# A three-pass graph kernel on one core: producers two blocks or groups ahead, node sums a block behind, sigmoid in place, and gather buffers that divide the number of groups

## The chip, the cores and the metric

The kernel runs on one core of a Trainium2 chip. The metric is the device time of one execution in microseconds (us); the median of 14 executions of the kernel before is 36074.31 us, the lowest 36034.74 and the highest 36114.28. Engines are named as in the profile: PE is TensorE (matmul), PEld its weight loads, DVE VectorE, ACT ScalarE, POOL GpSimd, SP SyncE.

## The reference, cut to what matters

Two layers of a graph network over 30,000 nodes with 128 features and 960,000 edges, which are sorted by destination. Everything is float32.

```python
def _rel_graph_conv(h, basis, coeff, bias, src, dst, etype, norm):   # R = 32 types, B = 8 bases
    W = jnp.einsum('rb,bdf->rdf', coeff, basis)
    Hr = jnp.einsum('nd,rdf->nrf', h, W)
    msg = Hr[src, etype] * norm
    return jax.ops.segment_sum(msg, dst, num_segments=N) + bias

h = relu(layernorm(x))
h1 = relu(_rel_graph_conv(h, basis1, coeff1, bias1, ...))
x = x + _rel_graph_conv(h1, basis2, coeff2, bias2, ...)

h = relu(layernorm(x))
for t in range(4):                       # 4 edge types
    k, q, v = h @ Wk[t] + bk[t], h @ Wq[t] + bq[t], h @ Wv[t] + bv[t]
    eta = jax.nn.sigmoid(k[dst] + q[src])
    msg = jnp.where((edge_type == t)[:, None], eta * v[src], 0.0)
    outs.append(segment_sum(msg, dst) + h @ Ws[t] + b[t])
x = x + mean(outs)
```

## The kernel before

The edges are walked three times: once for each of the two relational convolutions (passes c1 and c2, `rel_body`) and once for the gated layer (`gate_body`). Between c1 and c2 a short stage makes the node features of the second convolution, and between c2 and the gate another makes two tables: `ktab` with a key per node and type, and `qvtab` with query and value per node and type. Passes c1, c2 and the gate take nearly the whole span.

**Tiles, groups, blocks, stages.** A tile is 128 edges. `G` = 3 tiles are a group, whose destinations lie in one window of `W` = 32 nodes. `S` = 5 groups are a block, `SB` = 5 blocks a stage, `NQ` = 4 stages one iteration of the loop (`tc.For_i`): `NS` = 20 blocks, `NG` = 100 groups, 300 tiles. `NI` = 25 iterations make a pass. The body of an iteration is unrolled, and each engine keeps the order in which the code is written (`manual_schedule`), so a line that stands later in the text stands later in its engine's queue.

**Between the engines** there are only data dependencies and buffers: a tile name with `bufs=n` has n buffers that are used in turn, and whoever writes a buffer waits until all readers of its last content are done. The loop is the staggered kind: at each `stage_boundary()` (every fifth block) an engine may go on into the next stage only when all engines have passed `leave_stage()` of the stage that it is in, which stands at that stage's third block. An engine can so run at most 15 groups ahead across such a boundary, and across the end of an iteration.

**A group of the relational pass** (loop from L369). GpSimd gathers the rows of the three tiles' source nodes into `hg` (12 buffers), an indirect DMA of 128 rows each (helper, L107). VectorE makes for each tile a scatter matrix `sb` (L394, 9 buffers): one of 32 window columns per edge, times the edge's eight basis coefficients. TensorE multiplies `hg` with `sb` and adds the three tiles up in `pa` (L400, 3 buffers in PSUM). ScalarE copies `pa` into the block's `ab` (L404).

**Once per block**, written between the groups of that block:
- `types(s)` (L337): SP loads the edge types, 256 KB, into `er`.
- `onehot(s)`: VectorE compares them into `oh` (L344), TensorE multiplies by the coefficient table into `pc` (L347, one buffer).
- `coefficients(s)` (L356): VectorE multiplies `pc` with the edge weights into `ce`, which `sb` reads.
- `bases_out(s)` (L364): TensorE takes the block's `ab` through the eight bases into `po` (two buffers).
- `add_windows(po, base, s)` (L323): VectorE adds the five windows of `po` to the node sums `agg`, which stay in SBUF; the start columns come from registers that `bases` loads once per stage.

Before the change a block s has `types(s + 1)` at its start; `bases_out(s - 1)` after its second group; `add_windows` of block s - 1, `onehot(s + 1)` after its third; `coefficients(s + 1)` after its fourth.

**A group of the gate.** SP loads the keys of the group's window (`kw`, L437) and once per block the codes of the edges (`kb`, L429, 960 KB), which VectorE turns into one-hots in place (L441) along with `sel` (L446). `keys(n)`: TensorE picks each edge's key into `pk` (L453, 3 buffers in PSUM). GpSimd gathers query and value together into `qv` (9 buffers). VectorE adds the query to `pk` (L493), ScalarE takes the sigmoid into `eta` (L495, two buffers in PSUM), and `sums(n)` multiplies by the value into `msg` (L461) and adds to the block's `po` on TensorE (L463). At group n the text has, in order: the gathers of n, `keys(n + 1)`, the add and the sigmoid of n, `sums(n - 1)`; then, at the block's second group, `add_windows` of the block before, and at its third `onehot(s + 1)`.

Of the kernel before, what the change touches and what calls it, by code (L numbers as in the profile page):

```python
# [18 lines left out]
P = 128  # L19
# [44 lines left out]
def kernel(  # L64
# [210 lines left out]
    def sorted_path():  # L275
        with ExitStack() as all_:
# [48 lines left out]
            def rel_body(table, bas, cof):  # L325
                def body(i, io, pool, ps, iw, ic):
                    stage = {}
                    er, oh, pc, ce, ab, po, base = {}, {}, {}, {}, {}, {}, {}

                    def loads(k):  # L330
                        stage[k] = [stage_tile(io, "idx", src, I32, i, k),
                                    stage_tile(io, "relc", reld, F32, i, k),
                                    stage_tile(io, "nrm", norm, F32, i, k, 4 * TQ - S * G)]

                    def types(s):
                        er[s] = pool.tile([P, TQ, TP], I32, name="er")
                        nc.sync.dma_start(  # L337
                            er[s].rearrange("p c e -> p (c e)"),
                            bass.AP(tensor=et32_row.tensor, offset=(i * NG + s * S) * GE,
                                    ap=[[TQ * TP, 4], [0, R], [1, TQ * TP]]))  # L340

                    def onehot(s):
                        oh[s] = pool.tile([P, TQ, TP], F32, name="oh")
                        nc.vector.tensor_scalar(oh[s], er[s], icol4, None, op0=ALU.is_equal)  # L344
                        pc[s] = ps.tile([TP, TQ, 4, B], F32, name="pc", bufs=1)
                        for c in range(TQ):
                            nc.tensor.matmul(pc[s][:, c].rearrange("p q b -> p (q b)"),  # L347
                                             lhsT=oh[s][:, c, :],
                                             rhs=cof.rearrange("p q b -> p (q b)"),
                                             start=True, stop=True)  # L350

                    def coefficients(s):
                        ce[s] = pool.tile([TP, 4, TQ, B], F32, name="ce")
                        t0 = s % SB * S * G
                        nrm = stage[s // SB][2][:, t0:t0 + 4 * TQ]
                        nc.vector.tensor_mul(  # L356
                            ce[s], pc[s].rearrange("p c q b -> p q c b"),
                            nrm.rearrange("p (q c) -> p q c", q=4).unsqueeze(3).to_broadcast(
                                [TP, 4, TQ, B]))

                    def bases_out(s):
                        po[s] = ps.tile([P, S, W], F32, name="po")
                        for b in range(B):
                            nc.tensor.matmul(po[s].rearrange("p s w -> p (s w)"),  # L364
                                             lhsT=bas[:, b, :],
                                             rhs=ab[s][:, b].rearrange("p s w -> p (s w)"),
                                             start=(b == 0), stop=(b == B - 1))

                    loads(0)  # L369
                    types(0)  # L370
                    onehot(0)
                    coefficients(0)
                    for s in range(NS):
                        k = s // SB
                        if s % SB == 0:
                            if s:
                                tc.stage_boundary()
                            if k + 1 < NQ:
                                loads(k + 1)
                        if s % SB == 2:  # L380
                            leave_stage()
                        idx, relc, _ = stage[k]
                        if s + 1 < NS:
                            types(s + 1)
                        ab[s] = pool.tile([P, B, S, W], F32, name="ab")
                        for g in range(S):
                            t0 = (s % SB * S + g) * G
                            hg = pool.tile([TP, G, D], F32, name="hg", bufs=12)
                            for j in range(G):
                                gather(hg[:, j, :], table, idx[:, t0 + j:t0 + j + 1])  # L390
                            pa = ps.tile([P, B, W], F32, name="pa", bufs=3)
                            for j in range(G):
                                sb = pool.tile([TP, B, W], F32, name="sb", bufs=9)
                                nc.vector.scalar_tensor_tensor(  # L394
                                    sb, iw[:TP].unsqueeze(1).to_broadcast([TP, B, W]),
                                    relc[:, t0 + j:t0 + j + 1],
                                    ce[s].rearrange("p q c b -> p (q c) b")[
                                        :, g * G + j, :].unsqueeze(2).to_broadcast([TP, B, W]),
                                    op0=ALU.is_equal, op1=ALU.mult)
                                nc.tensor.matmul(pa.rearrange("p b w -> p (b w)"),  # L400
                                                 lhsT=hg[:, j, :],
                                                 rhs=sb.rearrange("p b w -> p (b w)"),
                                                 start=(j == 0), stop=(j == G - 1))
                            nc.scalar.copy(ab[s][:, :, g, :], pa)  # L404
                            if g == 1 and s:
                                bases_out(s - 1)
                            if g == 2 and s:
                                add_windows(po[s - 1], base[(s - 1) // SB], s - 1)
                            if g == 2 and s % SB == 0:
                                base[k] = bases(i, k, DVE)  # L410
                            if g == 2 and s + 1 < NS:
                                onehot(s + 1)
                            if g == 3 and s + 1 < NS:
                                coefficients(s + 1)
                    bases_out(NS - 1)
                    add_windows(po[NS - 1], base[NQ - 1], NS - 1)
                return body

            def gate_body(i, io, pool, ps, iw, ic):
                stage = {}  # L420
                kb, kw, sel, pk, qv, eta, po, base, kbase = {}, {}, {}, {}, {}, {}, {}, {}, {}

                def loads(k):
                    stage[k] = [stage_tile(io, *a, i, k) for a in (
# [14 lines left out]
                def onehot(s):  # L439
                    flat = kb[s].rearrange("p g e -> p (g e)")  # L440
                    nc.vector.tensor_tensor(flat, flat, ic.to_broadcast([P, S * G * TP]),  # L441
                                            ALU.is_equal)
                    sel[s] = pool.tile([TP, S * G, W], F32, name="sel")
                    t0 = s % SB * S * G
                    relc = stage[s // SB][1][:, t0:t0 + S * G]
                    nc.vector.tensor_tensor(  # L446
# [1 line left out]
                        relc.unsqueeze(2).to_broadcast([TP, S * G, W]), ALU.is_equal)  # L448

                def keys(n):  # L450
                    pk[n] = ps.tile([TP, G, D], F32, name="pk", bufs=3)
                    for j in range(G):
                        nc.tensor.matmul(pk[n][:, j, :], lhsT=kb[n // S][:, n % S * G + j, :],  # L453
                                         rhs=kw[n], start=True, stop=True)

                def sums(n):
# [1 line left out]
                    if g == 0:  # L458
                        po[s] = ps.tile([P, S, W], F32, name="po")
                    msg = pool.tile([TP, G, D], F32, name="msg", bufs=3)  # L460
                    nc.vector.tensor_mul(msg, eta[n], qv[n][:, :, 1, :])  # L461
                    for j in range(G):
                        nc.tensor.matmul(po[s][:, g, :], lhsT=msg[:, j, :],  # L463
                                         rhs=sel[s][:, g * G + j, :],
# [5 lines left out]
                    window(n)  # L470
                onehot(0)
                keys(0)
                for n in range(NG):
                    s, g, k = n // S, n % S, n // NGS
                    if n % NGS == 0:
# [7 lines left out]
                        types(s + 1)  # L483
                    if n + S < NG:
                        window(n + S)
                    qv[n] = pool.tile([TP, G, 2, D], F32, name="qv", bufs=9)
                    t0 = n % NGS * G
                    for j in range(G):
                        gather(qv[n][:, j].rearrange("p a f -> p (a f)"), qvtab,
                               stage[k][0][:, t0 + j:t0 + j + 1])  # L490
                    if n + 1 < NG:
                        keys(n + 1)
                    nc.vector.tensor_add(pk[n], pk[n], qv[n][:, :, 0, :])  # L493
                    eta[n] = ps.tile([TP, G, D], F32, name="eta")
                    nc.scalar.activation(eta[n], pk[n], AF.Sigmoid)  # L495
                    if n:
                        sums(n - 1)
                    if g == 1 and s:
                        add_windows(po[s - 1], base[(s - 1) // SB], s - 1)
                    if g == 1 and s % SB == 0:  # L500
                        base[k] = bases(i, k, DVE)
                    if g == 2 and s + 1 < NS:
                        onehot(s + 1)
                sums(NG - 1)
                add_windows(po[NS - 1], base[NQ - 1], NS - 1)

# [291 lines left out]
```

## Time and profile before

| | |
|---|---|
| median of 14 executions | 36074.31 us |
| the profiled execution's own time | 36086.58 us |
| its span | 36084.5 us |
| pass c1, first to last gather | 342.5 to 11827.2 us |
| pass c2 | 11973.0 to 23488.4 us |
| gate | 24384.0 to 35985.0 us |
| busy over the span: PE, PEld | 57%, 49% |
| DVE, ACT, POOL | 35%, 9%, 59% |
| mean granted clock of TensorE | 0.665 |

The profile is of one execution. A group of instructions is shown as `line engine operation out<-in shapes xcount | busy us, mean ns of one | idle us of the engine just before them, and what ended most of it`. A timeline line is `start us, us, engine, line, operation, tiles, xcount [idle before <- what ended it]`, with instructions of one kind that follow each other drawn together. A matmul of float32 leaves two records. A line of the waits is `engine, line <- what it waited for: us in all, times, longest`; "remote" there means that the profile names no instruction as the one that ended the wait. In a line of busy time by window, PEclk is the TensorE clock that was granted, as a share of full speed.

### The profile page before, as it was taken

To read this page: it belongs to the slowest core of one execution; us is meant where nothing else is said; L and a number is where in the kernel's file an instruction comes from. 1 tells how busy PE (TensorE), PEld (TensorE's weight loads), DVE (VectorE), ACT (ScalarE), POOL (GpSimd) and SP (SyncE) were. 2 spreads that over 40 slices of the span, in tenths; PEclk is the share of its full clock that TensorE was granted. 3 is DMA by queue.
4 is the path that set the end of the run, shared out by engine and by line. 5 is a ranking of instruction groups with operands and counts; after the bars stand their busy time and mean duration, and the time that the engine had idled before them with its cause. 6 is when DMAs were issued, how large, how long until landed. Compare 5 with 4: busy or idle time off the path is not lost. (4 is left out here: it accounts for less than half of the span.)

```text
span 36084.5 us, 310467 instructions
## 1 busy us (share of the span) xinstructions
PE 20420.6 (57%) x87057; PEld 17690.3 (49%) x87057; DVE 12806.5 (35%) x33126; ACT 3424.4 (9%) x8384; POOL 21253.4 (59%) x22512
## 2 busy tenths in 40 slices
PE   3555555555555555555555555585555555555555
PEld 2444444444444444444444444445555555555555
DVE  4333333333333333333333333363333333333333
ACT  1000000000000100000000000031111111111110
POOL 3666666666666566666666666606666666666665
PEclk8777777777777777777777777795555555555555
DMA  3222222222222222222222222254444444444444
GB/s 106 56 55 56 55 55 56 55 56 55 56 56 56 82 56 56 55 55 55 55 56 55 56 55 56 55 204 147 142 142 143 142 142 141 143 142 142 142 144 144
DMA packets 1707031, 3231.50 MB, mean 90 GB/s; under 512 B 540955, under 2 KB 955931, under 8 KB 1705582
## 3 DMA queue, kind: packets, MB, share of 16 engines
q0 software_dynamic: 840000, 1967.52, 20.0%
q1 hardware_dynamic: 787428, 1135.71, 9.4%
q10 hardware_dynamic: 78154, 109.64, 0.8%
q8 instruction: 825, 13.52, 0.2%
q14 instruction: 624, 5.11, 0.0%
HBM read 2968.58 MB, written 242.53 MB: 89 GB/s over the span
## 5 line engine op out<-in xcount | busy, mean ns | idle before, releaser
L107 POOL DMA_INDIRECT hg<-h,idx x15000 | 14164.1, 944 | 9322.0 <-issue 4340.7
L400 PE MATMUL pa<-sb,hg 128*128 128x256 f32 x30000 | 9260.9, 473 | 3469.9 <-ACT ab L404 1516.7
L107 POOL DMA_INDIRECT qv<-qvtab,qi x7500 | 7087.8, 945 | 5408.9 <-issue 3024.5
L400 PEld LDWEIGHTS pa<-sb,hg 128*128 128x128 f32 x30000 | 7121.5, 244 | 5011.8 <-ACT ab L404 1618.5
L394 DVE SCALAR_TENSOR_TENSOR sb<-cp,relc,ce 128x256 f32<-128x256 f32 x15000 | 6090.4, 474 | 403.2 <-remote 207.9
L463 PE MATMUL po<-sel,msg 128*128 128x32 f32 x15000 | 3488.4, 389 | 4710.4 <-DVE msg L461 3894.8
L463 PEld LDWEIGHTS po<-sel,msg 128*128 128x128 f32 x15000 | 3436.4, 329 | 5028.8 <-DVE msg L461 4093.7
L347 PE MATMUL pc<-coeff,oh 128*128 128x32 f32 x8000 | 1615.0, 359 | 6992.2 <-DVE oh L344 4795.3
L347 PEld LDWEIGHTS pc<-coeff,oh 128*128 128x128 f32 x8000 | 1499.4, 280 | 7366.4 <-DVE oh L344 4638.6
L323 DVE TENSOR_TENSOR agg<-agg,po 128x32 f32 x7500 | 1411.7, 188 | 10312.8 <-remote 7655.1
L453 PE MATMUL pk<-kw,kb 128*128 128x128 f32 x15000 | 4036.5, 443 | 134.0 <-DVE kb L441 118.4
L404 ACT COPY ab<-pa 128x256 f32<-128x256 f32 x5000 | 1842.8, 372 | 21252.9 <-PE pa L400 9047.1
L493 DVE TENSOR_TENSOR pk<-pk,qv 128x384 f32<-128x384 f32 x2500 | 1406.9, 563 | 6822.9 <-remote 4856.6
L453 PEld LDWEIGHTS pk<-kw,kb 128*128 128x128 f32 x15000 | 3479.0, 332 | 136.7 <-issue 136.7
L364 PE MATMUL po<-ab,basis 128*128 128x160 f32 x16000 | 2351.4, 300 | 48.3 <-issue 31.1
L364 PEld LDWEIGHTS po<-ab,basis 128*128 128x128 f32 x16000 | 2286.1, 191 | 119.2 <-issue 39.2
L495 ACT ACTIVATE eta<-pk 128x384 f32<-128x384 f32 x2500 | 1185.9, 475 | 10149.0 <-DVE pk L493 6548.7
L356 DVE TENSOR_TENSOR ce<-pc,nrm 128x128 f32<-128x128 f32 x1000 | 291.2, 291 | 4431.7 <-remote 3307.1
L461 DVE TENSOR_TENSOR msg<-eta,qv 128x384 f32<-128x384 f32 x2500 | 1367.3, 547 | 12.5 <-issue 10.4
L441 DVE TENSOR_TENSOR kb<-kb,cp 128x1920 f32<-128x1920 f32 x500 | 1072.1, 2144 | 39.5 <-issue 29.6
L344 DVE TENSOR_SCALAR oh<-er,icol 128x512 f32<-128x512 int32 x1000 | 517.7, 518 | 782.0 <-issue 758.7
L261 PE MATMUL pw<-wall,hT 128*128 128x512 f32 x1410 | 670.6, 612 | 74.8 <-ACT hT L255 74.8
(70 smaller groups left out, 2599.0 us busy)
## 6 DMA issues: line engine op xcount, KB each, us to landing
kb<-kcode SPq DMA_DIRECT2D x500, 960.0 KB
er<-in_et_row SPq DMA_DIRECT2D x1000, 256.0 KB
hg<-h,idx POOLq DMA_INDIRECT x15000
kw<-ktab SPq DMA_DIRECT2D x2500, 64.0 KB
qvtab<-qvt SPq DMA_DIRECT2D x235, 512.0 KB
qv<-qvtab,qi POOLq DMA_INDIRECT x7500
ktab<-kt ACTq DMA_DIRECT2D x235, 256.0 KB
xt<-in_x SPq DMA_DIRECT2D x47, 320.0 KB
```

Of the source, the lines that this page charges most:

```text
L107: nc.gpsimd.indirect_dma_start(out=to, out_offset=None, in_=table, in_offset=bass.IndirectOffsetOnAxis(ap=idx, axis=0))
L323: nc.vector.tensor_add(to, to, po[:, g, :])
L347: nc.tensor.matmul(pc[s][:, c].rearrange("p q b -> p (q b)"), lhsT=oh[s][:, c, :], rhs=cof.rearrange("p q b -> p (q b)"), start=True, stop ...
L364: nc.tensor.matmul(po[s].rearrange("p s w -> p (s w)"), lhsT=bas[:, b, :], rhs=ab[s][:, b].rearrange("p s w -> p (s w)"), start=(b == 0), ...
L394: nc.vector.scalar_tensor_tensor(sb, iw[:TP].unsqueeze(1).to_broadcast([TP, B, W]), relc[:, t0 + j:t0 + j + 1], ce[s].rearrange("p q c b - ...
L400: nc.tensor.matmul(pa.rearrange("p b w -> p (b w)"), lhsT=hg[:, j, :], rhs=sb.rearrange("p b w -> p (b w)"), start=(j == 0), stop=(j == G ...
L404: nc.scalar.copy(ab[s][:, :, g, :], pa)
L453: nc.tensor.matmul(pk[n][:, j, :], lhsT=kb[n // S][:, n % S * G + j, :], rhs=kw[n], start=True, stop=True)
L461: nc.vector.tensor_mul(msg, eta[n], qv[n][:, :, 1, :])
L463: nc.tensor.matmul(po[s][:, g, :], lhsT=msg[:, j, :], rhs=sel[s][:, g * G + j, :], start=(j == 0), stop=(j == G - 1))
L493: nc.vector.tensor_add(pk[n], pk[n], qv[n][:, :, 0, :])
L495: nc.scalar.activation(eta[n], pk[n], AF.Sigmoid)
```

## The change

In the relational pass `types` and `onehot` run two blocks ahead instead of one (with a second block in the prologue, and `er`, `oh` with three buffers and `pc` with two), and `coefficients(s + 1)` comes one group earlier. `onehot(s + 2)` follows the first group of block s, `coefficients(s + 1)` the third. `add_windows` is put off by a block: it adds block s - 2 after the fourth group of block s, and the last two blocks at the end. `hg` has 20 buffers instead of 12, `sb` 15 instead of 9; 20 divides the 100 groups of an iteration.

In the gate the keys run two groups ahead (`pk` has five buffers instead of three), the sigmoid writes back into `pk` and `eta` is gone, `sums` comes two groups behind instead of one, `onehot(s + 1)` after the block's second group, `add_windows` after its last. `qv` has 10 buffers instead of 9, which divides 100 too; `sel` has three.

```diff
 def types(s):
-    er[s] = pool.tile([P, TQ, TP], I32, name="er")
+    er[s] = pool.tile([P, TQ, TP], I32, name="er", bufs=3)
 def onehot(s):
-    oh[s] = pool.tile([P, TQ, TP], F32, name="oh")
+    oh[s] = pool.tile([P, TQ, TP], F32, name="oh", bufs=3)
-    pc[s] = ps.tile([TP, TQ, 4, B], F32, name="pc", bufs=1)
+    pc[s] = ps.tile([TP, TQ, 4, B], F32, name="pc")
...
 loads(0)
-types(0)
-onehot(0)
+for s in range(2):
+    types(s)
+    onehot(s)
 coefficients(0)
 for s in range(NS):
...
-    if s + 1 < NS:
-        types(s + 1)
+    if s + 2 < NS:
+        types(s + 2)
...
-        hg = pool.tile([TP, G, D], F32, name="hg", bufs=12)
+        hg = pool.tile([TP, G, D], F32, name="hg", bufs=20)
...
-            sb = pool.tile([TP, B, W], F32, name="sb", bufs=9)
+            sb = pool.tile([TP, B, W], F32, name="sb", bufs=15)
...
         nc.scalar.copy(ab[s][:, :, g, :], pa)
+        if g == 0 and s + 2 < NS:
+            onehot(s + 2)
         if g == 1 and s:
             bases_out(s - 1)
-        if g == 2 and s:
-            add_windows(po[s - 1], base[(s - 1) // SB], s - 1)
-        if g == 2 and s % SB == 0:
+        if g == 2 and s + 1 < NS:
+            coefficients(s + 1)
+        if g == 3 and s > 1:
+            add_windows(po[s - 2], base[(s - 2) // SB], s - 2)
+        if g == 3 and s % SB == 1:
             base[k] = bases(i, k, DVE)
-        if g == 2 and s + 1 < NS:
-            onehot(s + 1)
-        if g == 3 and s + 1 < NS:
-            coefficients(s + 1)
 bases_out(NS - 1)
-add_windows(po[NS - 1], base[NQ - 1], NS - 1)
+for s in (NS - 2, NS - 1):
+    add_windows(po[s], base[NQ - 1], s)

 # gate_body
-    sel[s] = pool.tile([TP, S * G, W], F32, name="sel")
+    sel[s] = pool.tile([TP, S * G, W], F32, name="sel", bufs=3)
...
-    pk[n] = ps.tile([TP, G, D], F32, name="pk", bufs=3)
+    pk[n] = ps.tile([TP, G, D], F32, name="pk", bufs=5)
...
-    nc.vector.tensor_mul(msg, eta[n], qv[n][:, :, 1, :])
+    nc.vector.tensor_mul(msg, pk[n], qv[n][:, :, 1, :])
...
 keys(0)
+keys(1)
 for n in range(NG):
...
-    qv[n] = pool.tile([TP, G, 2, D], F32, name="qv", bufs=9)
+    qv[n] = pool.tile([TP, G, 2, D], F32, name="qv", bufs=10)
...
-    if n + 1 < NG:
-        keys(n + 1)
+    if n + 2 < NG:
+        keys(n + 2)
     nc.vector.tensor_add(pk[n], pk[n], qv[n][:, :, 0, :])
-    eta[n] = ps.tile([TP, G, D], F32, name="eta")
-    nc.scalar.activation(eta[n], pk[n], AF.Sigmoid)
-    if n:
-        sums(n - 1)
-    if g == 1 and s:
+    nc.scalar.activation(pk[n], pk[n], AF.Sigmoid)
+    if n > 1:
+        sums(n - 2)
+    if g == 1 and s + 1 < NS:
+        onehot(s + 1)
+    if g == 4 and s:
         add_windows(po[s - 1], base[(s - 1) // SB], s - 1)
-    if g == 1 and s % SB == 0:
+    if g == 4 and s % SB == 0:
         base[k] = bases(i, k, DVE)
-    if g == 2 and s + 1 < NS:
-        onehot(s + 1)
+sums(NG - 2)
 sums(NG - 1)
 add_windows(po[NS - 1], base[NQ - 1], NS - 1)
```

## The prediction

> **What bounds the kernel now.** I read the page first, then busy time by pass, then the waits of VectorE, then single blocks in the timeline.
>
> ```profile
> span 36084.5 us, 310467 instructions
> L107 POOL DMA_INDIRECT hg<-h,idx x15000 | 14164.1, 944 | 9322.0 <-issue 4340.7
> L400 PE MATMUL pa<-sb,hg 128*128 128x256 f32 x30000 | 9260.9, 473 | 3469.9 <-ACT ab L404 1516.7
> L107 POOL DMA_INDIRECT qv<-qvtab,qi x7500 | 7087.8, 945 | 5408.9 <-issue 3024.5
> L323 DVE TENSOR_TENSOR agg<-agg,po 128x32 f32 x7500 | 1411.7, 188 | 10312.8 <-remote 7655.1
> L493 DVE TENSOR_TENSOR pk<-pk,qv 128x384 f32<-128x384 f32 x2500 | 1406.9, 563 | 6822.9 <-remote 4856.6
> ```
>
> GpSimd does nothing but gathers. VectorE waits long at two lines: the node sums (L323) and the add of the gate (L493). The three edge passes in the view of busy time by window (us, then PE, PEld, DVE, ACT, POOL busy, PEclk, DMA share, GB/s):
>
> ```profile
> 342.50:11827.20 11484.70, 6386.93 (x26873) 5381.73 (x26874) 3794.45 (x10950) 916.47 (x2488) 7081.45 (x7500) 0.73 0.21 56
> 11973.00:23488.40 11515.40, 6305.85 (x26873) 5331.38 (x26874) 3793.89 (x10951) 917.39 (x2488) 7082.68 (x7500) 0.72 0.21 56
> 24384.00:35985.00 11601.00, 6765.15 (x29915) 6444.68 (x29916) 4257.62 (x8474) 1214.70 (x2518) 7087.81 (x7500) 0.50 0.46 142
> ```
>
> No engine is full; the rest of the span is 1483 us. One iteration (25 per pass) takes 459 us in c1, 461 in c2, 464 in the gate. A gather is issued every 1.247 us (0.944 busy, 0.30 between), so 300 of them fill 374 us: the floor of an iteration. What is above it, 85 to 90 us, is time in which GpSimd stands. Its idle gaps by group give, per iteration: 16 to 17 us at the first gather, 6 to 7 in block 2, and in each of 17 other blocks one pause of 3.7 us (3.85 in the gate). Sum for c1: 374 + 17 + 6 + 17 x 3.7 = 460. One block of c1 in the timeline:
>
> ```profile
> 6104.66 0.94 POOL L107 DMA_INDIRECT hg<-h,idx  x1 [3.15 <-PE pc L347]
> 6104.76 7.00 PE L400 MATMUL pa<-sb,hg 128*128 128x256 f32 x24
> 6111.60 2.34 PE L364 MATMUL po<-ab,basis 128*128 128x160 f32 x16
> 6113.77 1.46 PE L400 MATMUL pa<-sb,hg 128*128 128x256 f32 x6
> 6121.68 1.07 DVE L323 TENSOR_TENSOR agg<-agg,po 128x32 f32 x5 [11.70 <-remote]
> 6123.38 1.91 PE L347 MATMUL pc<-coeff,oh 128*128 128x32 f32 x8 [8.15 <-DVE agg L323]
> 6126.16 0.29 DVE L356 TENSOR_TENSOR ce<-pc,nrm 128x128 f32<-128x128 f32 x1 [1.67 <-PE pc L347]
> 6126.23 0.94 POOL L107 DMA_INDIRECT hg<-h,idx  x1 [3.16 <-PE pc L347]
> ...
> 6330.43 0.94 POOL L107 DMA_INDIRECT hg<-h,idx  x1 [18.95 <-PE po L364]
> ...
> 6379.88 0.37 ACT L404 COPY ab<-pa 128x256 f32<-128x256 f32 x1 [43.70 <-remote]
> 6384.15 0.37 ACT L404 COPY ab<-pa 128x256 f32<-128x256 f32 x1 [3.90 <-PE pa L400]
> 6387.68 0.37 ACT L404 COPY ab<-pa 128x256 f32<-128x256 f32 x1 [3.15 <-remote]
> 6394.12 0.37 ACT L404 COPY ab<-pa 128x256 f32<-128x256 f32 x1 [6.08 <-remote]
> ```
>
> After a pause TensorE does five groups and the block's `po` (16 records, ended at 6113.94) in 10 us. The node sums that need this `po` start only at 6121.68, 7.7 us later, while GpSimd issues without a break. Behind them on VectorE stand the one-hot, `pc` and the coefficients. So a completion of TensorE reaches its waiters at once for 6 to 8 us after a pause of GpSimd, then late, and is let go about 2.5 us after GpSimd next stops (6120.88 + 0.94 to 6126.23 is such a stop). The last four lines are 60 us into gathering without a pause: a group each 3.5 to 6.4 us, against 3.74 at which GpSimd issues. So a block is cleared per pause, and VectorE waits for TensorE twice in series in each (L323, then L356):
>
> ```profile
> DVE agg L323 <- remote: 3720.5, 307, 18.2
> DVE ce L356 <- remote: 1629.7, 179, 47.6
> ```
>
> (c1: us, times, longest; all waits of L323 and L356 over 1 us come to 4748 and 2012 us.)
>
> **The change, part by part.**
>
> *Iteration ends.* 100 groups modulo 12 buffers is 4: the first group of an iteration writes the buffer of group 96, one of the last. So GpSimd waits for nearly the whole drain (18.95 us at 6330.43). With 20 buffers it writes that of group 80. In the gate 9 becomes 10: group 90 instead of 99. Of 17 and 16 us I keep 4; bounds 0 and 17.
>
> *Producers.* `types`, one-hot and `pc` a block further ahead are the same instructions (oh 0.518 us, pc 1.1 to 1.9, one 256 KB load on SP). `ce` then reads a `pc` that was issued seven groups, 26 us, earlier (now one), and the sums of L323 a `po` seven groups old (now one). The late completions seen are 7 us typically and 18.2 at most at L323, 47.6 at most at L356: nearly all fits. The two waits in series leave VectorE, and 15 `sb` tiles let it run five groups ahead. The prologue has one load, one one-hot and one `pc` more before the first coefficients: 0 to 7 us per iteration; GpSimd's lead, up to 15 groups (56 us) by the stage rule, hides it, so 0; without that cover 50 x 7 = 350 us. New waits: `bases_out` on TensorE needs the `po` of two blocks back to be added, `pc` that of two blocks back to be read; both come three groups or more before, so nothing queues behind them. The base registers (four loads an iteration on VectorE) move one place with the sums: 0.
>
> *What is late next* is `hg`'s release by the pa matmuls, TensorE's completion itself. Let the consumers clear 6 groups in 10 us around each pause (five and a `po` now, one more since nothing stops them there), and then one per r us. A pause every N groups needs 10 + r(N - 6) = 3.7 + 3.74 N. The spacing of the four copies averages 4.75 us, so N = 22; the longest, 6.4, gives 12; two late completions of 4 us per group give 10. I take 12, as `po` and `pc` also queue there. An iteration: 374 + 100/12 x 3.7 (31) + 4 = 409; 50 of them 20,450 us (now 23,000).
>
> *Gate.* In-place sigmoid: the same 0.475 us on ScalarE and 0.547 us `msg`, so nothing; the two banks of `eta` become two more `pk`. Keys come two groups ahead, the sums a group later, and the lead of the gathers over the adds stays 8 groups (9 - 1, 10 - 2). Node sums at the block's end instead of its second group: L323 waits only 201 us in the whole gate, so at most that is gained; 0 taken. The one-hot (2.14 us, L441) comes a group, 3.7 us, earlier. In the block looked at its 960 KB load was issued 15.7 us before it, which leaves 12; each us by which it were late would cost up to 500 us in all; 0 taken. Here TensorE works at clock 0.50 and takes 2.56 us per group, so 4 groups in 10 us, and two completions, each 3.5 to 4 us apart when late, make r = 7.5: 10 + 7.5(N - 4) = 3.85 + 3.74 N, N = 6.3 (now 5). An iteration: 374 + 16 x 3.85 (61) + 4 = 439; 25 are 10,975 (now 11,601). Bounds: N = 5 (451 us) and N = 14 (402).
>
> *A rule against it.* In 4 us windows of that block the granted clock is 1.00 between 6108 and 6116, and 0.50 from 6120 to 6128, after TensorE stood still from 6116 to 6120; 24 pa records take 7.00 us at the lower end and 5.43 (6323.72) at the upper. The Trainium skill, TensorE: Matmul & The Clock Gate, HAM oscillation, says that a wait of over some 3.4 us puts TensorE back at half clock. By it, shorter gaps would leave the clock up and c be better than I sum. But the gate stands at 0.50 throughout, 58% busy, with gaps mostly shorter than that: the row doesn't bear it out, and an evenly fed c can go cold. That is the third rival.
>
> *Sum:* 20,450 + 10,975 + 1,483 = 32,908; the profiled execution's own time is 2 us over its span (36,086.6), and it is 12 above the median: 32,900.
>
> **Rivals.**
>
> 1. *Completions keep up, GpSimd nearly without a pause.* For it: the spacings of 3.5 and 4.3 us in the quoted copies are near 3.74. Against: 6.4, and the gate's 7 to 8. N = 35 in c (374 + 11 + 2 = 387) and about 15 in the gate (399): 19,350 + 9,975 + 1,473 (rest, less 10 as above) = 30,800.
> 2. *One pause per block stays;* the waits only move from L323 and L356 to the pa and pk completions. For it: in all three passes, with different waits, a pause comes every five groups and ends on TensorE. Only the iteration ends gain: 374 + 20 x 3.7 = 448 and 374 + 77 = 451, so 22,400 + 11,275 + 1,473 = 35,150.
> 3. *Slower: TensorE cold in c.* Fed evenly rather than in bursts, its clock stays at 0.50 as in the gate; a group then takes 3.57 us, so 10 us after a pause hold 2.8 groups, not 6. At r = 8, 10 + 8(N - 2.8) = 3.7 + 3.74 N, N = 3.8: 374 + 97 + 4 = 475 in c; with the gate as now 23,750 + 11,601 + 1,473 = 36,820. It decides once N in c falls below 4.5 (over 22 pauses an iteration). Against: at r = 5.6, N is 5, which is rival 2.
> 4. *It doesn't act:* the stage rule (a lead of 15 groups at most at each fifth block), not the 20 buffers, ends the lead, or cold clock and saved ends cancel: about 36,070.
>
> **How the numbers follow.** The sum with N from 10 to 22: 0.45 (own range 32,000 to 33,700, gate bounds in it). Rival 1: 0.20; rival 2: 0.18; rival 3: 0.13; rival 4: 0.04. The range reaches from just under rival 1 to just over rival 2, 30,600 to 35,400, and leaves out rivals 3 and 4. 0.2% is 72 us, about what a measurement can tell from no change. Faster 0.83, same 0.04, slower 0.13.
>
> **What would show it.** Right: the first gather of an iteration waits under 5 us; VectorE's waits of over 1 us at the sums and the coefficients fall from 6760 us in c1 to under 1500; GpSimd pauses 8 times an iteration in c, 16 in the gate, each still 3 to 4 us; its busy share rises from 59% to 65%. Wrong: as many pauses as blocks (rival 2), pauses more often with PEclk near 0.50 in c (rival 3), or none (rival 1); and the sum fails if the stop itself, 3.7 us, changes its length.

## The result, and the profile after

The changed kernel takes 35,709.9 us (median of 6 executions, 35,682.9 to 35,753.4) against 36,074.9 before (28 executions): a ratio of 0.9901, 95% interval 0.9891 to 0.9911. That is 365 us faster, about 1%, where 3,170 were forecast; the measured time lies above the range. The profiled execution has a span of 35,714.6 us.

The same groups on the page after (busy, mean ns, idle just before them, and what ended most of it); the last line is that of `sb` on the page before:

```profile
span 35714.6 us, 314060 instructions
L107 POOL DMA_INDIRECT hg<-h,idx x15000 | 14194.9, 946 | 9188.9 <-issue 4812.1
L395 DVE SCALAR_TENSOR_TENSOR sb<-cp,relc,ce 128x256 f32<-128x256 f32 x15000 | 6488.6, 478 | 13423.0 <-remote 7496.6
L107 POOL DMA_INDIRECT qv<-qvtab,qi x7500 | 7089.4, 945 | 5138.8 <-issue 3142.4
L496 DVE TENSOR_TENSOR pk<-pk,qv 128x384 f32<-128x384 f32 x2500 | 1402.8, 561 | 6727.2 <-remote 4736.5
L323 DVE TENSOR_TENSOR agg<-agg,po 128x32 f32 x7500 | 1396.9, 186 | 1772.8 <-remote 949.3
...
L394 DVE SCALAR_TENSOR_TENSOR sb<-cp,relc,ce 128x256 f32<-128x256 f32 x15000 | 6090.4, 474 | 403.2 <-remote 207.9
```

VectorE's idle time before the node sums (L323) fell from 10,312.8 to 1,772.8 us, and that before `sb` (L394 before, L395 now) rose from 403.2 to 13,423.0. In c1, waits of over 1 us at sums and coefficients fell from 6,760 to 723 us; at `sb` they rose from 262 to 6,216. So the waits moved to another line, and GpSimd's idle time hardly changed (9,322.0 to 9,188.9 at `hg`). The three passes (busy time by window; columns as before):

```profile
343.80:11792.10 11448.30, 6690.84 (x26825) 5498.52 (x26825) 3890.98 (x10931) 887.47 (x2481) 7098.17 (x7500) 0.73 0.21 56
11943.50:23386.00 11442.50, 6655.97 (x26824) 5489.90 (x26824) 3883.71 (x10931) 883.99 (x2481) 7096.74 (x7500) 0.73 0.21 56
24296.50:35614.20 11317.70, 6824.52 (x29911) 6448.46 (x29911) 4189.36 (x8470) 1214.51 (x2518) 7089.44 (x7500) 0.51 0.47 146
```

c1 gained 36 us, c2 73, the gate 283. One block of c1 after, in the timeline (lines of TensorE, VectorE, ScalarE):

```profile
6105.07 4.05 PE L401 MATMUL pa<-sb,hg 128*128 128x256 f32 x18
...
6112.68 0.48 DVE L395 SCALAR_TENSOR_TENSOR sb<-cp,relc,ce 128x256 f32<-128x256 f32 x1 [7.61 <-remote]
...
6116.90 0.92 ACT L405 COPY ab<-pa 128x256 f32<-128x256 f32 x3 [13.47 <-remote]
...
6117.33 2.93 PE L401 MATMUL pa<-sb,hg 128*128 128x256 f32 x6 [8.21 <-ACT ab L405]
```

TensorE does three groups (18 records, ended at 6109.12) and stands: its three `pa` banks are full until ScalarE copies them, and ScalarE hears of them only at 6116.90, when all three come at once. VectorE stands at `sb` for completions of the same matmuls. (A completion is the signal by which TensorE tells a waiting engine that a matmul is done.) GpSimd's pauses in the c1 of after, where an iteration begins, at block 4 and at block 5:

```profile
5833.85 0.94 POOL L107 DMA_INDIRECT hg<-h,idx  x1 [11.40 <-PE po L364]
...
5928.68 0.94 POOL L107 DMA_INDIRECT hg<-h,idx  x1 [12.23 <-PE pc L347]
...
5955.88 0.94 POOL L107 DMA_INDIRECT hg<-h,idx  x1 [8.52 <-PE pa L401]
```

With the blocks of an iteration counted from 0, c1's idle time above the 0.30 us between gathers is now 8.6 us at the first group of an iteration (16.9 before), but 8.1, 4.8 and 5.8 at the three other stage boundaries (0.5 or less before) and 10.1 at the start of block 4, where the twenty buffers are used up. All pauses of an iteration come to 82 us against 85.

### The profile page after: what moved, and what is told of

Read it like the earlier page. It is cut to its first block, busy times and chain, and to the rows that moved or that the text cites. A ratio compares the mean times of both kernels' runs of the same rounds, so it can differ in the third digit from the quotient of the medians.

```text
span 35714.6 us, 314060 instructions
## 1 busy us (share of the span) xinstructions
PE 21149.2 (59%) x87057; PEld 17986.4 (50%) x87057; DVE 12936.2 (36%) x33126; ACT 3367.0 (9%) x8384; POOL 21285.8 (60%) x22512
## 5 line engine op out<-in xcount | busy, mean ns | idle before, releaser
L107 POOL DMA_INDIRECT hg<-h,idx x15000 | 14194.9, 946 | 9188.9 <-issue 4812.1
L401 PE MATMUL pa<-sb,hg 128*128 128x256 f32 x30000 | 9446.4, 465 | 6531.5 <-issue 4157.4
L395 DVE SCALAR_TENSOR_TENSOR sb<-cp,relc,ce 128x256 f32<-128x256 f32 x15000 | 6488.6, 478 | 13423.0 <-remote 7496.6
L401 PEld LDWEIGHTS pa<-sb,hg 128*128 128x128 f32 x30000 | 6745.2, 233 | 8487.8 <-issue 5061.1
L364 PE MATMUL po<-ab,basis 128*128 128x160 f32 x16000 | 3187.5, 362 | 2721.9 <-issue 2105.5
L455 PE MATMUL pk<-kw,kb 128*128 128x128 f32 x15000 | 4131.2, 438 | 981.8 <-issue 860.2
L364 PEld LDWEIGHTS po<-ab,basis 128*128 128x128 f32 x16000 | 2995.8, 241 | 3020.1 <-issue 2335.3
L497 ACT ACTIVATE pk<-pk 128x384 f32<-128x384 f32 x2500 | 1185.8, 475 | 9599.0 <-DVE pk L496 5684.8
L323 DVE TENSOR_TENSOR agg<-agg,po 128x32 f32 x7500 | 1396.9, 186 | 1772.8 <-remote 949.3
L347 PE MATMUL pc<-coeff,oh 128*128 128x32 f32 x8000 | 1298.0, 316 | 493.5 <-DVE oh L344 467.0
L463 DVE TENSOR_TENSOR msg<-pk,qv 128x384 f32<-128x384 f32 x2500 | 1364.8, 547 | 89.7 <-remote 87.9
L261 PEld LDWEIGHTS pw<-wall,hT 128*128 128x128 f32 x1410 | 249.4, 190 | 360.5 <-issue 169.7
```

The costliest lines, as they stand in the source:

```text
L107: nc.gpsimd.indirect_dma_start(out=to, out_offset=None, in_=table, in_offset=bass.IndirectOffsetOnAxis(ap=idx, axis=0))
L323: nc.vector.tensor_add(to, to, po[:, g, :])
L364: nc.tensor.matmul(po[s].rearrange("p s w -> p (s w)"), lhsT=bas[:, b, :], rhs=ab[s][:, b].rearrange("p s w -> p (s w)"), start=(b == 0), ...
L395: nc.vector.scalar_tensor_tensor(sb, iw[:TP].unsqueeze(1).to_broadcast([TP, B, W]), relc[:, t0 + j:t0 + j + 1], ce[s].rearrange("p q c b - ...
L401: nc.tensor.matmul(pa.rearrange("p b w -> p (b w)"), lhsT=hg[:, j, :], rhs=sb.rearrange("p b w -> p (b w)"), start=(j == 0), stop=(j == G ...
L463: nc.vector.tensor_mul(msg, pk[n], qv[n][:, :, 1, :])
```

## The experiments

The runs fell on different chips, and these turned out to be of two kinds: on some, TensorE's completions come late as in the trace of before (the kernel before takes 35,980 to 36,160 us there); on two others they come promptly (29,770 and 29,830). Each time is compared with the kernel before on its own chip. The theories changed as results came in; a name in a quoted text holds for that experiment.

**What makes the completions late: gathers, matmuls, or their width** (kernels made from the one after; late chip, before 36,158 us).

One gather per group:
```diff
-for j in range(G):
-    gather(hg[:, j, :], table, idx[:, t0 + j:t0 + j + 1])
+gather(hg[:, 0, :], table, idx[:, t0:t0 + 1])     # all tiles read hg[:, 0]; the same for qv
```


> The kernel after with one gather per group instead of three (all three tiles of a group use the rows of the first; the other rows are left out). All else is issued as before: 27 matmuls per block in c, 30 in the gate. Three theories. Theory 1: TensorE has done its work in time, but its completions reach the waiters late while GpSimd issues gathers, about one per 1.3 to 2 us, and the rest in GpSimd's pauses. Then with a third of the gathers the passes fall to TensorE's own pace of 1.8 to 2.6 us per group: 200 to 280 us per iteration instead of 458 (c) and 452 (gate), the whole 17,000 to 22,000 us. Theory 2: TensorE (or a consumer behind it) really takes 4.5 us per group, whatever GpSimd does: the passes stay near 11,400 us each, the whole over 34,000. Theory 3: the lead of the gathers (buffers, stage rule) is what binds: pauses stay at about 80 us per iteration, 125 + 80, and VectorE no longer waits for TensorE.

18,874 us, ratio 0.522 (0.520 to 0.524), inside theory 1's range. Its c1:

```profile
340.10:5700.00 5359.90, 4996.34 (x26799) 4508.05 (x26800) 3732.82 (x10924) 904.11 (x2481) 2364.66 (x2500) 0.96 0.20 58
```

TensorE is 93% busy at clock 0.96. From the end of a group's last `pa` record to ScalarE's copy it is 0.61 us on average, where the c1 of after has 7.35. So neither TensorE nor VectorE is slow by itself: the lateness needs the steady gathers. It isn't the DMA load as a whole (58 GB/s here, 56 in the c1 of after); whether it is GpSimd's issuing or the transfers that it starts, this run can't tell. Theory 2 falls. Theory 3's 205 us per iteration is near the 214 measured, but it is TensorE's work that fills them, not pauses for want of buffers.

One basis, two halves, double width:
```diff
-for b in range(B):                      # t_one_base
+for b in range(1):
...
+for c in (slice(0, H), slice(H, 2 * H)):   # t_halves: two matmuls of 80 columns each
...
-rhs=ab[s][:, b].rearrange("p s w -> p (s w)"),           # t_wide
+rhs=ab[s][:, b].rearrange("p s w -> p (s w)").unsqueeze(1).to_broadcast([P, 2, S * W]),
```


> The kernel after with one of the eight basis matmuls per block in c1 and c2 (the other seven are left out): 20 matmuls per block instead of 27, 400 instead of 540 per iteration. Theory 1: in the trace of after 40% of the completions of c1 come in GpSimd's pauses (216 of 540 in 82 us, 2.6 per us) and 324 while it issues; 400 would need 76 in pauses, 29 us: 403 us per iteration instead of 458, c1 and c2 near 10,100 us each, the whole near 33,000. Theory 2: TensorE's time of some 2 to 3 us per block goes, 410 to 420 per iteration, 33,700 to 34,000. Theory 3: no change, 35,700.

> The kernel after with each basis matmul split into two of 80 columns: the same products, 35 matmuls per block instead of 27 (700 per iteration). Theory 1: 160 more completions at 2.6 per us in pauses are up to 62 us more per iteration, the whole up to 38,800 us; at least half of that. Theory 2: only TensorE's overhead of the eight more matmuls, 1 to 2.5 us per block, and the same for the next kernel. Theory 3: no change.

> The kernel after with each basis matmul over 320 columns instead of 160 (the block's columns twice; the second copy isn't used): the same 27 matmuls per block, with about 2 to 3 us more work of TensorE per block. Theory 1: the number of completions is the same, so under 1% (35,500 to 36,000). Theory 2: as much as the halves, 1.5 us or more per block, 37,200 or more. Theory 3: no change.

One base 35,203 us (0.974, interval 0.971 to 0.976), halves 36,042 (0.996, 0.995 to 0.998), wide 35,870 (0.992, 0.989 to 0.995). After, at its ratio of 0.9901, would take 35,800 us on this chip; against that they are -600, +240 and +70 us; with 1,000 blocks in c1 and c2, -0.6, +0.2 and +0.1 us per block. The wide one can't be told from the kernel after (the two intervals overlap). The signs of the other two are those of theory 1, the sizes a quarter or less of what it named (-2,800 for one base, up to +3,100 for the halves). So counting completions doesn't give the time. A reason may be that most of them pass around a pause, where they are cheap; that is argued.

**Buffers and `pa` banks, first on chips with prompt completions** (before 29,768, then 29,826 us).

```diff
 # buffers: the kernel before
-hg bufs=12, qv bufs=9
+hg bufs=20, qv bufs=10
 # oldbufs: the kernel after
-hg bufs=20, qv bufs=10
+hg bufs=12, qv bufs=9
 # pa2 / pa6: the kernel after
-pa = ps.tile([P, B, W], F32, name="pa", bufs=3)
+pa = ps.tile([P, B, W], F32, name="pa", bufs=2)            # pa2
+if (s * S + g) % 2 == 0:                                  # pa6: two groups to a bank
+    pa2 = ps.tile([P, 2, B, W], F32, name="pa", bufs=3)
+pa = pa2[:, (s * S + g) % 2]
```


> The kernel before with the buffer counts alone: hg 20 instead of 12, qv 10 instead of 9 (sums still one group behind, one block of producers ahead). Theory A: what the change gained is the gate's end of an iteration alone (16.0 us before the first gather, 1.96 after; 25 x 14 = 350 us) and it comes from 10 dividing 100: so the gate falls to 11,250 to 11,350 us here too, and c1 and c2 stay within 100 us of 11,485 and 11,515 or fall a little; the whole 35,650 to 35,850. Theory B: the gain comes from the producers and sums further apart: no change here, over 36,000. In both the first gather's wait in the gate falls below 5 us.

> The kernel after with the old buffer counts, hg 12 and qv 9, all else as in the change (the sums two groups behind, so the gathers' lead over the adds is seven groups). Theory A: the gate's wait at the first gather is back near 16 us and the gate near 11,600 or above; c within 1% of after; the whole 35,950 to 36,250. Theory B: within 0.3% of after, 35,600 to 35,820.

> The kernel after with two pa buffers in PSUM instead of three. Theory P: while GpSimd issues, completions of TensorE come late, so per pause TensorE gets as far as it can without being answered, and that is the number of pa buffers (after three groups its next matmul waits for ScalarE's copy, which waits for the late completion). With two buffers it gets a group less far per pause, 4 instead of 5 groups: pauses 25% more, 82 to about 105 us per iteration in c, c1 and c2 each 11,900 to 12,300, the whole 36,600 to 37,300. Theory Q: the pauses hang on something else (gather buffers, stage rule, GpSimd's own queue): within 0.5% of after.

> The kernel after with two groups in each pa bank: three banks, six groups of 1 KB per partition instead of three, all else the same. Theory P: TensorE gets two to three groups further per pause, 7 to 8 instead of 5: pauses 82 to 50 us per iteration in c or fewer, c1 and c2 near 10,500 to 10,900 each, the whole 33,900 to 34,800. Theory Q: within 0.5% of after, 35,550 to 35,900.

> The kernel before with hg 20 and qv 10 alone. With late completions: theory A (the gain is the gate's end of an iteration, by 10 dividing 100) 35,650 to 35,850 us, the gate at 11,250 to 11,350; theory B (the gain is the order) over 36,000. With prompt completions 29,630 again.

> The kernel after with hg 12 and qv 9. With late completions: theory A 35,950 to 36,250 us, the gate back at 11,600 or above; theory B 35,600 to 35,820. With prompt completions 29,800 again.

> The kernel after with two pa buffers, once more for the same reason. With late completions: theory P 36,600 to 37,300 us; theory Q 35,550 to 35,900. With prompt ones 29,600 to 29,660 by both.

> The kernel after with six groups in three pa banks, once more, since in the run before this one the chip answered promptly (the kernel before took 29,770 us there and GpSimd hardly paused), so that nothing could be told of the pauses. If the completions are late again (the kernel before near 36,100 us): theory P (TensorE gets per pause as many groups further as it has pa buffers) 33,900 to 34,800 us, c1 and c2 at 10,500 to 10,900; theory Q (the pauses hang on something else) 35,550 to 35,900. If the kernel before is near 29,770 again, 29,600 to 29,660 by both.

| | first chip | second chip | ratio (second chip) |
|---|---|---|---|
| buffers | 29,631 | 29,693 | 0.9955 (0.9937 to 0.9972) |
| oldbufs | 29,800 | 29,846 | 1.0006 (0.9995 to 1.0016) |
| pa2 | 29,619 | 29,667 | 0.9945 (0.9925 to 0.9964) |
| pa6 | 29,621 | 29,670 | 0.9948 (0.9928 to 0.9967) |

Here c1 takes 9,367 to 9,398 us, 375 to 376 us per iteration, whatever the kernel: it is gather-bound. The one thing left to gain is the gate's end of an iteration: 9,599 us with `qv` 9 and 9,421 to 9,469 with 10 (first chip). So there the whole of the half per cent is `qv` 10, and the order gives nothing. (The kernel after itself was not timed on these chips; pa2 and pa6 differ from it in `pa` alone.) For the late chips these runs decide nothing, and the kernel with two `pa` buffers was not run on one.

**The same on a chip with late completions** (before 35,979 us).

> The changed kernel as it is. Where the kernel before takes some 36,100 us (late completions): 35,700 again. Where it takes 29,800 (prompt): the passes are gather-bound and only the gate's end of an iteration is left to gain, 25 x 6 us of 29,800: 29,620 to 29,680, as its variants with two and six pa groups gave.

> The kernel after with six groups in three pa banks. With late completions: theory P (TensorE gets per pause as many groups further as it has pa buffers) 33,900 to 34,800 us, c1 and c2 at 10,500 to 10,900; theory Q (the pauses hang on something else) 35,550 to 35,900. With prompt ones as the kernel after.

> The kernel before with hg 20 and qv 10 alone. With late completions: theory A (the gain is the gate's end of an iteration, by 10 dividing 100) 35,650 to 35,850 us, the gate at 11,250 to 11,350; theory B (the gain is the order) over 36,000. With prompt ones 29,630 to 29,690.

After again 35,719 us, 0.9926 (0.9907 to 0.9945). Six `pa` groups 36,189, slower than before (1.006, 1.004 to 1.008): theory P falls, and theory Q's range is missed as well. In its c1 a pause of 2 to 3.4 us is followed by 4.4 copies until the next, against 4.7 with three groups on this chip, and 3.6 pauses per iteration are over 8 us long, against 2.2; why more room makes it slower stays open. The buffer counts alone 36,902, 1.026 (1.024 to 1.028): theory A falls. Theory B's "over 36,000" came true, but with a loss of some 920 us that it didn't foresee. The same program on the two kinds of chip by window, first its c1 on the second chip with prompt completions:

```profile
344.30:9726.40 9382.10, 6796.33 (x26980) 4942.07 (x26980) 3908.34 (x10995) 930.91 (x2499) 7096.57 (x7500) 0.84 0.26 68
```

and its c1 and gate on the chip with late ones:

```profile
344.90:12280.30 11935.40, 6410.32 (x26799) 5388.41 (x26800) 3824.11 (x10918) 909.95 (x2482) 7108.92 (x7500) 0.73 0.19 54
...
25319.40:36837.30 11517.90, 6802.45 (x29904) 6453.97 (x29904) 4247.01 (x8473) 1213.96 (x2518) 7109.15 (x7500) 0.50 0.46 143
```

The same gathers with the same busy time (7,097 and 7,109 us), and 2,553 us more. Against the profile of before, `hg` 20 without the new order costs 451 us in c1 and 462 in c2, and the gate gains 83.

**The lead of the gathers** (late chip, before 36,104 us).

```diff
 # hg10: the kernel after
-hg = pool.tile([TP, G, D], F32, name="hg", bufs=20)
+hg = pool.tile([TP, G, D], F32, name="hg", bufs=10)
```


> The kernel after with hg 10 instead of 20, all else the same. With late completions: theory L (it is the length of the lead; short pauses clear more groups per us of pause): the pauses at stage ends and of the wrap go, all pauses at about 0.6 us per group as the short ones of after have it, 60 us per iteration instead of 82: 434 us per iteration, c1 and c2 near 10,850 each, the whole 34,300 to 34,900. Theory M (the order and the lead only shift the same pause time about): c1 and c2 within 100 us of 11,440, the whole 35,600 to 35,900; or above, since a shorter lead hides less. The gate as in after, 11,320. With prompt completions (kernel before near 29,800): within 0.2% of after, 29,600 to 29,700.

> The kernel after with hg 12 and qv 9. With late completions: theory L: c1 and c2 near 11,100 each (short pauses at 0.6 us per group, but the wait of 17 us at each iteration's first gather stays), and the gate, with 9 buffers that don't divide 100, back near 11,600: the whole 35,200 to 35,600. Theory M: c1 and c2 at 11,440 or above, the whole over 35,800. With prompt completions 29,800 to 29,850.

`hg` 10: 34,768 us, 0.9627 (0.9611 to 0.9643); `hg` 12 with `qv` 9: 35,091, 0.9718 (0.9702 to 0.9734). Theory L holds, in the size it named (with 12 buffers 110 us better than that, in the gate). The kernel after with ten buffers is 3.7% faster than the kernel before on such a chip, where the change as made gained 0.7 to 1.0%. Its passes, with the c1 of 12 buffers first:

```profile
342.30:11410.70 11068.40, 6869.95 (x26909) 5424.56 (x26910) 3874.56 (x10971) 885.79 (x2490) 7096.70 (x7500) 0.73 0.22 58
...
343.50:11328.00 10984.50, 6898.65 (x26916) 5505.41 (x26917) 3889.12 (x10973) 885.37 (x2491) 7105.08 (x7500) 0.74 0.22 58
...
23343.30:34680.90 11337.60, 6815.53 (x29920) 6441.09 (x29921) 4193.10 (x8478) 1215.46 (x2520) 7109.83 (x7500) 0.51 0.47 146
```

With `hg` 10 GpSimd's idle time above the gaps is 2.6 to 3.4 us in every block of an iteration but block 2 (8.0). The profiles with late completions that differ in order and buffers alone, in one table (us; they come from several chips, and the kernel after, profiled on two, differs by at most 10 us per pass):

| order | hg | c1 | c2 | qv | gate |
|---|---|---|---|---|---|
| before | 12 | 11,485 | 11,515 | 9 | 11,601 |
| before | 20 | 11,935 | 11,977 | 10 | 11,518 |
| after | 20 | 11,448 | 11,443 | 10 | 11,318 |
| after | 12 | 11,068 | 11,078 | 9 | 11,486 |
| after | 10 | 10,985 | 10,995 | 10 | 11,338 |

"Order" here is all of the change but `hg` and `qv`: producers and sums further apart, and 15 `sb` tiles, which no run takes apart. It gives 416 to 437 us per pass of c at 12 buffers and 487 to 535 at 20. The 20 buffers cost 364 to 462 us per pass with either order. That is where c's gain went.

## Why the prediction was wrong, step by step

*What bounds the kernel* was read rightly: gathers of 1.25 us, and on top the pauses in which late completions are let out. t_third shows that it takes the steady gathers to make them late; where they are prompt, the kernel before already runs at 29,770 us, below even rival 1's 30,800. One example was misread: a further gather ran from 6122.13 to 6123.07, so the node sums at 6121.68 started before the stop, not after it. Of the 500 node sums of that c1, 153 start in a pause. The 2.5 us fit ScalarE's copies better: those in a pause start 3.0 us (median) after the last gather's end, 95 of 100 at 2.3 us or later.

*The waits of VectorE* went as forecast (under 1,500 us at sums and coefficients: 723). The point after it failed: *what is late next*. The prediction lets the consumers clear 6 groups in the 10 us around a pause, then one per 6.4 us, and so has a pause each 12 groups. Counting ScalarE's copies in c1 by the time since GpSimd resumed after a pause of over 2 us:

| | before | after |
|---|---|---|
| us per copy, first 8 us | 2.7 | 3.3 |
| 8 to 15 us | 12.3 | 6.1 |
| later, the next pause included | 6.1 | 5.4 |

In the prediction's own terms: in the 10 us from the start of a pause there are 3.7 copies after the change (3.4 before), where 6 were taken; and from then to the next pause it is 8.4 us per copy, where 6.4 were taken. The 6 groups are the term that was mis-sized most: with 3.7 in their place its equation gives N = 6.5 instead of 12, and with 8.4 as well, 10 + 8.4 (N - 3.7) = 3.7 + 3.74 N, N = 5.3. The trace has 18.2 pauses of over 2 us per iteration, one each 5.5 groups, where 8 were named; GpSimd's busy share is 60%, not 65%. The five groups of the block that the prediction quotes were more than most pauses let through. So c1 and c2 took 458 us per iteration instead of 409, which is 2,440 of the 2,810 us that the forecast was short; the gate is 340 more.

Why so few groups pass is argued, not isolated: in the timeline above TensorE starts a window with completions still owed and stands after three groups (more `pa` groups alone made it slower).

*Iteration ends.* In the gate the 16.0 us of an iteration's first block became 2.0 (4 forecast): right. But the gate's pauses stayed at 3.75 us per block where N = 6.3 had been taken (18.3 of over 2 us per iteration, 16 named); 453 us per iteration, 439 forecast, and no run here takes that apart. (The 2.56 us of TensorE per group stand in no row; its busy time in the gate before is 2.71 per group.) With `qv` 10 and the old order the end's gain is partly given back: the first wait goes too (1.1 us), yet block 2 waits 12.0 us instead of 6.8 and the pass gains only 83 us. In c the first gather waits 8.6 us, not under 5. The stage rule, which the prediction had only as a part of rival 4, ends the lead of 20 buffers: 8.6, 8.1, 4.8 and 5.8 us at the four boundaries, and 10.1 at block 4, where 4 in all were kept. With 10 and with 12 buffers the three inner boundaries have 0.1 us or less.

*What was costed at nothing and wasn't:* the longer lead itself. The prediction held the 20 buffers for cover that could at worst be useless. By length of pause, idle time per group cleared until the next pause (c1): after the change 0.6 us for pauses of 2 to 3.4 us, 0.9 for 6 to 9, 1.3 for 9 to 13; before it 0.8 for the short ones and 1.5 for the 18 us at an iteration's start. A long lead hardly changes how many pauses there are (with the old order 22.8 of over 2 us per iteration at `hg` 12 and 22.4 at 20; with the new one 19.1 and 18.2), but makes more of them long and dear: over 8 us there are 1.0 per iteration at 12 buffers with either order, 2.3 after the change, 3.7 with the buffers alone and 0.4 with `hg` 10. The step from pauses to time, "N groups per pause of 3.7 us", lacked that a pause's length changes; the prediction had named this as what would make the sum fail.

*Rivals.* By its time rival 4 is nearest (36,070; the measured time is 360 us less), by what happened rival 2: the waits moved to the `pa` and `pk` completions, with a pause about every five groups. Rival 2's 35,150 is 560 us less than the measured time, nearly all of it in c, 458 us per iteration where it has 448. There the four stage boundaries and block 4 cost 37 us per iteration, against 18 for five pauses of 3.7, and the other 15 blocks some 10 us less than by that rival.

Rival 3 didn't come on these chips: c's clock is 0.72 to 0.73 before, 0.73 after and 0.74 in the c1 of `hg` 10. The clock rule (the Trainium skill, TensorE: Matmul & The Clock Gate, HAM oscillation) has a wait of over some 3.4 us put TensorE back at half clock. Its case hardly arose here: TensorE waited that long 21 times per iteration of c1 before and 17 times after. On a chip with prompt completions it did arise, and the trace doesn't bear the rule out: with the old order (b_buffers) c1 has 4.0 such waits per iteration and clock 0.85, with the new one (b_oldbufs) 0.3 and 0.77. So an evenly fed c did lose clock, as rival 3 feared, but at no cost worth naming, since gathers bound it there (9,367 and 9,389 us).

By the Trainium skill, Perfetto Trace Analysis, Tensor Engine Instruction, a matmul's end in the profile is an estimate from its size, and its semaphore goes out only when PSUM has acknowledged. The traces agree in so far as a waiter starts 0.04 us after the record's end or 15 us after it (below).

## What to carry to other kernels

Before costing a wait that you move, count over the whole pass how much the consumers clear per pause, and use that number instead of one block's. More buffers ahead of a bottleneck are not free where running ahead is itself what delays the answers: try a lead that is shorter, divides the loop, and stays inside the stage rule. Buffer counts and order should be measured apart (here +910 us in c for 20 buffers with the old order, and -1,020 for the order with 20 buffers), and a kernel bound by such lateness may be bound by something else on the next chip.

## What the runs showed of the hardware

The same program (the order before, `hg` 20, `qv` 10) took 29,693 us on one chip and 36,902 on another, with the same pitch of gathers (1.25 us). From the end of the `po` records to the node sums it was 0.04 us at the 5th and at the 95th percentile on the first, and 0.04, 1.18 (median) and 15.4 (95th) on the second; from the `pa` records to ScalarE's copy 0.05 us on average against 5.06. The kernel before took 36,158, 35,979 and 36,104 us on three chips, 29,768 and 29,826 on two. Each of them was visited once, so that these runs don't tell the chip from the occasion, and what distinguishes the two kinds isn't shown.

While the completions are late, TensorE itself can go one record at a time. In the run with `hg` 10, from 11 us after GpSimd began to issue until it paused (timeline, the first of these records and the gather after the pause):

```profile
6109.77 0.30 PE L364 MATMUL po<-ab,basis 128*128 128x160 f32 x1 [0.81 <-issue]
6111.19 0.30 PE L364 MATMUL po<-ab,basis 128*128 128x160 f32 x1 [1.12 <-issue]
6112.59 0.43 PE L364 MATMUL po<-ab,basis 128*128 128x160 f32 x1 [1.10 <-issue]
...
6123.51 0.95 POOL L107 DMA_INDIRECT hg<-h,idx  x1 [3.35 <-PE pa L401]
```

One record each 1.40 to 1.42 us, with nothing that the profile shows to wait for ("issue"), where the 16 records of one `po` took 2.34 us in the block of before. VectorE's `sb` start at 6109.08, 6111.91 and 6114.72 in the same stretch, two such steps apart. What this step is made of inside the chip stays open.
